# Gram matrices in two column halves, bias sums on GpSimd, and fewer filler steps in the first entry, in a four-layer convolution and attention kernel

## The chip, the cores and the metric

The kernel runs on one core of a Trainium2 chip. The metric is the device time in microseconds (us) of one execution, given as a median over runs. A profile of one execution is there too: a record of what each engine did. The engines are TensorE (PE; its weight loads are shown apart as PEld), VectorE (DVE), ScalarE (ACT), GpSimd (POOL) and SyncE (SP, which issues the transfers).

## The reference, cut to what matters

The input `x` is 8 batches of 512 channels by 1024 pixels in fp32. Four layers follow one another:

```python
# layer 0, MID = 64 channels: attention scaled by its largest singular value
f = relu(batchnorm(conv1x1(x, Wf, bf)))        # [8, 64, 1024]
g = relu(batchnorm(conv1x1(x, Wg, bg)))
h = conv1x1(x, Wh, bh)
z = einsum('bcn,bcm->bnm', f, g)
sigma = svd(z)[0]
x = x + conv1x1(einsum('bnm,bcm->bcn', z / sigma, h), Wv, bv)
# layer 1: group norm, attention with wq, wk, wv, wp, and x added
# layer 2: nonlocal attention over 128 channels, batch norm, and x added
# layer 3: 1x1 convolution of signs, batch norm, x added, a shifted PReLU
```

The kernel never forms `z`. Its singular values follow from the two 64x64 Gram matrices `f fT` and `g gT` of a batch, and `h zT` needs only `g hT`, also 64x64. Two batches make a pair: their 64 channels lie side by side on the 128 partitions. For the four pairs there are twelve Gram matrices of 128x128, of which only the two 64x64 blocks on the diagonal (one for each batch) have a meaning; the blocks off the diagonal would mix two batches.

## The kernel before, in words

**Stage 1, to about 100 us.** The 1x1 convolutions of layer 0 run for all eight batches (L1248), with statistics for the batch norm. Each batch is read in; two of them stay resident.

**Weight preparation and first entry, about 100 to 195 us.** This is where the change lies. Its pieces:

- `natural` (L1214) transposes the weights q, k, v. `product` (L1288) multiplies two of them: `wu` from k and q, and `wo` from p and v. A filler step of it is one 128x128 by 128x512 fp32 product, which the profile shows as two records[...].
- `relu` (L1370, on ACT) finishes f and g of a batch. `turned_pair` and `turn` (transposes at L1142, copies on ACT at L1146 and on DVE at L1148) turn a pair so that pixels lie on the partitions, in 8 tiles.
- `gram` (L1342) sums over the 8 tiles: eight 128x128 products of full width into a wide PSUM tile, with one `yield` after four. DVE multiplies the result with `mask2`, which zeroes the off-diagonal blocks, into `gm[j][:, i, :]` (L1351).
- `chain` finds the singular value of a pair by repeated squaring. Each step is two 128x128 products (`products`, L1029 and L1030), an eviction (L1043 to L1051), and now and then a trace sum (`total`, L1060) whose reciprocal scales the next eviction. The first pair's chain, `chain(jl, True)`, runs here; `jl` is pair 3, for batch 6 is the first in the order.
- `scale_z` makes a tile `rep` under the tag `absw` and reads it in four products with the identity (shown at L1202).
- `biases` makes two row vectors, `bu` and `bo`. It makes a tile `part` under the same tag `absw`; with it each weight's four tiles are scaled by a bias column and summed on DVE (one L1313 and three L1315 each), and then four products with a column of ones (L1322) sum over the partitions. `bo` also goes into `bvo`, which every entry adds.
- `sums_u` makes the Strassen-Winograd sums of `wu`.

All but the first pair's own steps are strung together in one generator, `filler()`, called `todo`. Its order is: natural v, product wu, Gram matrix 2 of the first pair, scale_z, then for the three other pairs their turns and Gram matrices with the steps of `biases` and `sums_u` taken in between, then product wo. A `yield` ends a filler step. The main body takes steps from `todo` by `next(todo)`: five at first, then after every step of the first chain one, two or four, then in the first batch's entry `entering(0)` by the list (2, 3, 3, 3, 4, 4, 6), and then what is left.

**What sets the order.** In the block with `tc.manual_schedule` PE's instructions run in just the order in which the program writes them; a wait of one holds up all that follow. DVE, ACT and POOL also run their own queues in order.

**The first entry** (`entering(0)`, which goes through `enter`): L290 makes the first batch's weights `pv` from a Gram tile; four visits, each of two products into two banks (L412) and on DVE, for each bank, an add (L421), statistics (L424), and once a visit an aggregate (L426). Then the group sums L433, small DVE steps, L440, a reciprocal root (L233 to L235, with a power on POOL), eight scalings of the batch into `h` (L463), and two sums `hs` for the Strassen-Winograd products (L327, L328). From there the main loop starts: its product terms at L388 are of `h` with `wu` and of `hs` with `su`. The chains of the other pairs run inside the main loop, between its products.

Of the kernel before, what the change touches and what calls it, by code (L numbers as in the profile page):

```python
# [8 lines left out]
F32 = mybir.dt.float32  # L9
# [3 lines left out]
ALU = mybir.AluOpType  # L13
# [3 lines left out]
P = 128  # L17
B = 8
C = 512
N = 1024  # L20
CC = C // P
NT = N // P
# [3 lines left out]
MID = 64  # L26
# [59 lines left out]
def kernel(  # L86
# [17 lines left out]
    nc = tc.nc  # L104
    mm = nc.tensor.matmul
# [11 lines left out]
    def wide():  # L117
        return psum["wide"].tile([P, N], F32, tag="wide", name="wide")
# [4 lines left out]
    def bank():  # L123
        return psum["bank"].tile([P, HF], F32, tag="bank", name="bank")
# [20 lines left out]
    def side(i):  # L145

        return slice(i * MID, (i + 1) * MID)
# [13 lines left out]
    a1 = early.enter_context(tc.tile_pool(name="a1", bufs=1))  # L161
# [10 lines left out]
    def block_ones(size, value, name):  # L172

        n = P // size
        member = const.tile([P, n], F32, tag=name + "_m", name=name + "_m")
        nc.vector.tensor_reduce(
            member, ident.rearrange("p (g j) -> p g j", j=size), AX.X, ALU.add
        )
        t = const.tile([P, n, size], F32, tag=name, name=name)
        nc.vector.tensor_scalar(  # L180
            t, member.unsqueeze(2).to_broadcast([P, n, size]), value, None, ALU.mult
        )
        return t.rearrange("p g j -> p (g j)")

    mask2 = block_ones(MID, 1.0, "mask2")
# [36 lines left out]
    def vec(name):  # L222
        return ct[:, COL[name] : COL[name] + CC]
# [20 lines left out]
    r_dram = [dram.tile([4, N // 4], F32, name=f"r_dram{i}") for i in range(2 * B)]  # L244
    f_dram = [dram.tile([P, HF], F32, name=f"f_dram{b}") for b in range(B)]
    gm = [keep.tile([P, 3, P], F32, tag=f"gm{j}", name=f"gm{j}") for j in range(NPAIR)]
    sw3 = wpool.tile([P, CC, C // 2], F16, tag="sw3", name="sw3")
    round3 = const.tile([P, 1], F32, tag="round3", name="round3")
    nc.gpsimd.memset(round3, ROUND)
# [616 lines left out]
    def entering(n):  # L866

        b = order[n]
        f = load_f(b)

        def steps():
            while b // 2 not in ready:
                next(behind)
            if b % 2 == 0:
                for i in (b, b + 1):
                    pvs[i] = weights0(i)
            yield
            yield from enter(resident[b], f, pvs.pop(b), 2 if n else CC)

        return steps()  # L880
# [423 lines left out]
    def biases():  # L1304

        part = a1.tile([P, 2, C], F32, tag="absw", name="part")
        for j, (w, v) in enumerate(((nat["k"], vec("L1_conv_bq")), (sbw["p"], bvc))):
            t = part[:, j, :]  # L1310
            for k in range(CC):
                if k == 0:
                    nc.vector.tensor_scalar(t, w[:, 0, :], v[:, 0:1], None, ALU.mult)  # L1313
                else:
                    nc.vector.scalar_tensor_tensor(  # L1315
                        t, w[:, k, :], v[:, k : k + 1], t, ALU.mult, ALU.add
                    )
                yield False
        for j, dst in enumerate((bu, bo)):
            ps = bank()  # L1320
            for i in range(CC):
                mm(  # L1322
                    out=ps[:, i : i + 1],
                    lhsT=part[:, j, bass.ts(i, P)],
                    rhs=ones1,
                    start=True,
                    stop=True,
                )
            if dst is bu:
                nc.vector.tensor_copy(bu, ps[:, 0:CC])  # L1330
            else:
                nc.vector.tensor_tensor(bo, ps[:, 0:CC], vec("L1_conv_bp"), ALU.add)
            yield True
        nc.vector.tensor_tensor(bvo, bo, vec("L0_conv_bv"), ALU.add)
# [2 lines left out]


    def gram(j, i, lt, rhs):
        ps = wide()  # L1340
        for t in range(NT):
            mm(  # L1342
                out=ps[:, 0:P],
                lhsT=lt[:, t, :],
                rhs=rhs[:, t, :],
                start=t == 0,
                stop=t == NT - 1,
            )
            if t == NT // 2 - 1:
                yield  # L1350
        nc.vector.tensor_tensor(gm[j][:, i, :], ps[:, 0:P], mask2, ALU.mult)  # L1351
        yield

    def turned_pair(j):
# [7 lines left out]
    def grams(j):  # L1362
        for ft, gt in turned_pair(j):
            yield
        for i, lt, rhs in ((0, ft, ft), (1, gt, gt), (2, ht_pair[j], gt)):
            yield from gram(j, i, lt, rhs)

    def relu(b, i):
        t = (fs, gs)[i][b]
        nc.scalar.activation(t, t, AF.Relu, bias=bi0[:, i : i + 1], scale=sc0[:, i : i + 1])  # L1370
        if i == 0:
            nc.sync.dma_start(out=f_dram[b], in_=t)
# [10 lines left out]
    ps = bank()  # L1383
# [5 lines left out]
    ps = bank()  # L1389
# [35 lines left out]
    def filler():  # L1425

        yield from natural("v", "k")
        load_w("p", w_p, [P, CC, C], a1, tag="v")  # L1430
        yield from product(nat["q"], nat["k"], wu, True)
        yield from gram(jl, 2, ht_pair[jl], gtl)
        scale_z()
        yield
        between = biases()
        sums = sums_u()
        for j in rest:
            for _ in grams(j):
                next(sums, None)
                yield  # L1440
                if next(between, None):
                    yield
        yield from product(nat["v"], sbw["p"], wo, False)

    todo = filler()
# [3 lines left out]
        pass  # L1449
    for i, t in ((0, ftl), (1, gtl)):  # L1450
        for _ in gram(jl, i, t, t):
            pass

    relus = iter([(2 * j + k, i) for j in rest for i in range(2) for k in range(2)])
    with tc.manual_schedule(engines={mybir.EngineType.PE}):
        steps = entering(0)
        for k, _ in enumerate(chain(jl, True)):

            for _ in range(4 if k == 3 * NSTEP + 3 else 2 if k % 3 == 1 or k == 0 else 1):
                next(todo, None)  # L1460
            for args in (next(relus, None),):
                if args:
                    relu(*args)
        for n in (2, 3, 3, 3, 4, 4, 6):
            next(steps)
            for _ in range(n):
                next(todo, None)
        for _ in todo:
            pass
# [195 lines left out]
```

## Time and profile before

| | us |
|---|---|
| median of three runs | 1898.24 |
| lowest, highest | 1897.3, 1898.89 |
| span of the profiled execution | 1896.9 |

In the profiled execution the mean granted clock of PE is 0.998 of full speed. Busy times over the span are given in the page's first part; here are those groups of the stretch that the change touches.

| group | count | where |
|---|---|---|
| L1342, Gram products | 192 records, one every 111.6 ns within a group | 109 to 171 us |
| L1029 and L1030, first chain | pairs of records, 0.38 us a product | 114 to 158 us |
| L1288, wu and wo | 0.86 us a product | 103 to 187 us |
| L412, the entry's products | four groups of 1.13 us | 161 to 174 us |

How to read the lines: "PE" is the engine, "L1342" the line of the kernel, then the operation, what it writes and what it reads, and for a timeline the start and the length in us first and the idle time before it, with what ended it, last. In a timeline neighbouring instructions of one kind are drawn together with a count, and the length of such a group is from the start of its first to the end of its last. In the list of groups the numbers after the bar are the busy time in us, the mean of one instruction in ns, and the idle time of the engine just before.

### The profile page before, as it was taken

What the parts mean: (1) busy time and instruction counts of PE and PEld (TensorE: products, weight loads), DVE (VectorE), ACT (ScalarE), POOL (GpSimd) and SP (SyncE); (2) the same over time, 40 slices, a digit from 0 to 9 for tenths busy, and PEclk for the clock granted to TensorE, in tenths of its full rate; (3) what the DMA queues carried; (4) which work ended last, traced back from release to release, by engine and by line L of the source; (5) the groups of instructions that cost most, each with busy time, mean ns of one, the idle gap of its engine ahead of it and who ended that gap; (6) DMA issues with size and microseconds to landing.
All of it is one profiled execution on the core that took longest, in us unless ns stands there. A gap on an engine that the chain in (4) does not pass through costs nothing.

```text
span 1896.9 us, 16376 instructions
## 1 busy us (share of the span) xinstructions
PE 1878.3 (99%) x6178; PEld 976.1 (51%) x6178; DVE 1097.5 (58%) x1762; ACT 511.4 (27%) x811; POOL 225.7 (12%) x176
## 2 busy tenths in 40 slices
PE   9999999999999999999999999999999999999997
PEld 3366556544745446444645446544645455544653
DVE  3256576448664677338663675457753775466547
ACT  2142222034312432035202421144202521234013
POOL 0000111201121011200121001200130011101121
PEclk9999999999999999999999999999999999999999
DMA  8420000002000020002000110002000200000001
GB/s 314 168 78 6 1 6 12 1 12 89 17 1 0 34 72 12 1 12 89 18 0 0 42 65 12 0 23 78 12 1 12 89 12 0 1 34 22 12 0 47
DMA packets 25203, 66.52 MB, mean 35 GB/s; under 512 B 3552, under 2 KB 4764, under 8 KB 24476
## 3 DMA queue, kind: packets, MB, share of 16 engines
q1 hardware_dynamic: 24188, 64.96, 9.4%
q8 instruction: 51, 0.84, 0.2%
q10 hardware_dynamic: 864, 0.43, 0.1%
q14 instruction: 36, 0.29, 0.0%
q0 software_dynamic: 64, 0.00, 0.0%
HBM read 46.44 MB, written 18.94 MB: 34 GB/s over the span
## 4 chain that ended last, share of the span: by engine, by line
PE 98%; DVE 1%; ACT 0%; DMA 0%; issue 0%; POOL 0%; ACTq 0%; DVEq 0%
PE bank L388 46%; PE bank L557 20%; PE bank L958 6%; PE bank L806 6%; PE bank L1248 5%; PE bank L658 3%; PE bank L675 3%; PE bank L412 2%; PE bank L698 1%; PE wide L1288 1%; PE bank L1029 1%; PE wide L1342 1%; PE bank L1030 1%; PE quad L1142 1%; PE bank L829 0%; PE bank L1060 0%
## 5 line engine op out<-in xcount | busy, mean ns | idle before, releaser
L557 PE MATMUL bank<-e,vt 128*128 128x512 f32 x768 | 333.8, 592 | 0.0
L557 PEld LDWEIGHTS bank<-e,vt 128*128 128x128 f32 x768 | 145.0, 190 | 175.4 <-issue 173.4
L388 PE MATMUL bank<-ut,h 128*128 128x512 f32 x384 | 182.3, 597 | 0.0
L345 DVE TENSOR_TENSOR e<-bank,e 128x512 f32<-128x512 f32 x128 | 87.8, 686 | 81.0 <-PE bank L388 80.3
L388 PE MATMUL bank<-us,hs 128*128 128x512 f32 x256 | 121.5, 597 | 0.3 <-DVE us L317 0.3
L388 PEld LDWEIGHTS bank<-ut,h 128*128 128x128 f32 x384 | 71.4, 190 | 95.6 <-issue 84.5
L958 PE MATMUL bank<-e,tpg 128*128 128x512 f32 x256 | 114.7, 595 | 0.0
L806 PE MATMUL bank<-tpg 128*128 128x512 f32 x256 | 114.6, 592 | 0.0
L813 ACT ACTIVATE e<-bank 128x512 f32<-128x512 f32 x128 | 76.4, 597 | 128.5 <-PE bank L806 128.5
L360 POOL TENSOR_TENSOR e<-e 128x512 f32<-128x512 f32 x32 | 44.2, 1381 | 412.5 <-ACT e L339 144.1
L388 PE MATMUL bank<-wo,h 128*128 128x256 f32 x384 | 91.9, 382 | 0.0
L388 PE MATMUL bank<-h,wu 128*128 128x512 f32 x192 | 90.4, 593 | 0.1
L818 DVE TENSOR_TENSOR esum<-esum,e 128x1024 f32<-128x1024 f32 x48 | 58.8, 1225 | 54.5 <-ACT e L813 54.5
L345 DVE TENSOR_TENSOR vt<-bank,vt 128x512 f32<-128x512 f32 x64 | 44.1, 689 | 65.5 <-PE bank L388 64.7
L806 PEld LDWEIGHTS bank<-tpg 128*128 128x128 f32 x256 | 48.6, 190 | 60.7 <-issue 60.5
L958 PEld LDWEIGHTS bank<-e,tpg 128*128 128x128 f32 x256 | 48.1, 190 | 60.4 <-issue 60.3
L388 PEld LDWEIGHTS bank<-wo,h 128*128 128x128 f32 x384 | 71.6, 190 | 11.5 <-issue 2.5
L360 POOL TENSOR_TENSOR ut<-ut 128x512 f32<-128x512 f32 x16 | 21.8, 1365 | 465.3 <-ACT ut L341 465.3
L388 PEld LDWEIGHTS bank<-us,hs 128*128 128x128 f32 x256 | 47.1, 190 | 52.9 <-issue 47.8
L686 ACT ACTIVATE sg<-xt,rb 128x512 f16<-128x512 f32 x64 | 45.3, 718 | 100.7 <-DVE xt L677 97.1
L1248 PE MATMUL bank<-xt,fg 128*64 128x512 f32 x256 | 59.9, 616 | 4.4 <-DMA fg<-in_w_fg 4.4
L658 PEld LDWEIGHTS bank<-tpg,xt 128*128 128x128 f32 x512 | 59.5, 192 | 7.2 <-issue 7.2
(333 smaller groups left out, 2968.1 us busy)
## 6 DMA issues: line engine op xcount, KB each, us to landing
xt<-in_x SPq DMA_DIRECT2D x55, 512.0 KB
out<-both SPq DMA_DIRECT2D x63, 256.0 KB
rfull<-r_dram SPq DMA_DIRECT2D x15, 512.0 KB
f_dram<-f SPq DMA_DIRECT2D x8, 256.0 KB
fb<-f_dram SPq DMA_DIRECT2D x8, 256.0 KB
w<-in_w SPq DMA_DIRECT2D x1, 1024.0 KB
q<-in_w_q SPq DMA_DIRECT2D x1, 1024.0 KB
k<-in_w_k SPq DMA_DIRECT2D x1, 1024.0 KB
```

What stands on the lines that cost most here:

```text
L345: nc.vector.tensor_tensor(dst, ps, u, ALU.add)
L360: nc.gpsimd.tensor_tensor(c22, c22, c12, ALU.add)
L388: mm(out=ps[:, q * w : (q + 1) * w], lhsT=lt(ka, kb, q, k), rhs=rhs(ka, kb, q, k), start=first and q == 0 and k == 0, stop=last and k == 1 ...
L557: mm(out=ps, lhsT=a[:, t, bass.ts(r_, P)], rhs=e[t], start=first and t == 0, stop=last and t == NTH - 1, skip_group_check=True,)
L658: mm(out=ps[:, i, :], lhsT=xt[:, cc, bass.ts(4 * h + i, P)], rhs=sbw["tpg"][:, cc, 2 * P : 3 * P], start=cc == 0, stop=cc == CC - 1,)
L675: mm(out=ps, lhsT=sbw["z"][:, bass.ts(oc, P)], rhs=att, start=True, stop=True)
L686: nc.scalar.activation(sg[:, cc, :], xt[:, cc, half(h)], AF.Sign, bias=rb3[:, cc : cc + 1])
L806: mm(out=ps, lhsT=pt[:, 0, bass.ts(t, P)], rhs=tt[:, 0, half(h)], start=True, stop=True,)
L813: nc.scalar.activation(e[:, half(h)], ps, AF.Exp, scale=float(P) ** -0.5)
L818: nc.vector.tensor_tensor(esum, esum, e, ALU.add)
L958: mm(out=banks[h], lhsT=gt[:, t, :], rhs=es[t][:, half(h)], start=t == 0, stop=t == NT - 1,)
L1248: mm(out=banks[i][side(h), :], lhsT=w0[i][:, cc, :], rhs=xt[:, cc, half(h)], start=cc == 0, stop=cc == CC - 1,)
```

## The change

There are four parts.

1. `gram` takes one bank instead of a wide tile. For each of the eight tiles it issues two 64x64 products, one for each batch of the pair, into its own half of the array's columns and of the bank's partitions. It has no `yield` halfway. The two diagonal blocks are copied to `gm`, one by DVE and one by ACT. The off-diagonal blocks of `gm` are zeroed once, by four memsets on POOL at the start.
2. Around the first pair's own two Gram matrices the loop takes a step from `todo` after each.
3. `biases` scales and sums on POOL: a scaling into a tile `term`, with one buffer, and an add. It yields once for each weight, not once for each of its tiles.
4. The list of filler steps in the first entry is (1, 2, 2, 2, 2, 3, 4), 16 in all, where it was 25.

```diff
     gm = [keep.tile([P, 3, P], F32, tag=f"gm{j}", name=f"gm{j}") for j in range(NPAIR)]
+    for g in gm:
+        nc.gpsimd.memset(g[:, 0:2, :].rearrange("p i c -> p (i c)"), 0.0)
...
             for k in range(CC):
-                if k == 0:
-                    nc.vector.tensor_scalar(t, w[:, 0, :], v[:, 0:1], None, ALU.mult)
-                else:
-                    nc.vector.scalar_tensor_tensor(
-                        t, w[:, k, :], v[:, k : k + 1], t, ALU.mult, ALU.add
-                    )
-                yield False
+                to = a1.tile([P, C], F32, tag="term", name="term") if k else t
+                nc.gpsimd.tensor_scalar(to, w[:, k, :], v[:, k : k + 1], None, ALU.mult)
+                if k:
+                    nc.gpsimd.tensor_tensor(t, t, to, ALU.add)
+            yield False
...
     def gram(j, i, lt, rhs):
-        ps = wide()
+
+        ps = bank()
         for t in range(NT):
-            mm(
-                out=ps[:, 0:P],
-                lhsT=lt[:, t, :],
-                rhs=rhs[:, t, :],
-                start=t == 0,
-                stop=t == NT - 1,
-            )
-            if t == NT // 2 - 1:
-                yield
-        nc.vector.tensor_tensor(gm[j][:, i, :], ps[:, 0:P], mask2, ALU.mult)
+            for k in range(2):
+                mm(
+                    out=ps[side(k), 0:MID],
+                    lhsT=lt[:, t, side(k)],
+                    rhs=rhs[:, t, side(k)],
+                    start=t == 0,
+                    stop=t == NT - 1,
+                )
+        for k in range(2):
+            to, of = gm[j][side(k), i, side(k)], ps[side(k), 0:MID]
+            if k:
+                nc.scalar.copy(to, of)
+            else:
+                nc.vector.tensor_copy(to, of)
         yield
...
         for _ in gram(jl, i, t, t):
-            pass
+            next(todo)
...
-        for n in (2, 3, 3, 3, 4, 4, 6):
+        for n in (1, 2, 2, 2, 2, 3, 4):
```

## The prediction

> **What bounds the kernel now.** I read first the page's busy shares and its chain of work that ended last:
>
> ```profile
> PE 1878.3 (99%) x6178; PEld 976.1 (51%) x6178; DVE 1097.5 (58%) x1762; ACT 511.4 (27%) x811; POOL 225.7 (12%) x176
> ...
> PE 98%; DVE 1%; ACT 0%; DMA 0%; issue 0%; POOL 0%; ACTq 0%; DVEq 0%
> ```
>
> TensorE is the bound over the whole span; all its idle time is 1896.9 − 1878.3 = 18.6 us. So PE work taken away is gained, unless PE then waits. The change touches only 109 to 191 us (weight preparation and the first batch's entry), so I read that stretch next, in the timeline of PE (start, us, instruction, count of records, idle before):
>
> ```profile
> 109.24 2.03 PE L1342 MATMUL wide<-ft 128*128 128x128 f32 x16
> 111.75 2.02 PE L1342 MATMUL wide<-gt 128*128 128x128 f32 x16 [0.47 <-DVE gm L1351]
> 114.15 0.49 PE L1029 MATMUL bank<-gm 128*128 128x128 f32 x2 [0.39 <-DVE gm L1351]
> ...
> 133.74 1.06 PE L1202 MATMUL bank<-ident,rep 128*128 128x128 f32 x8
> ...
> 158.43 1.13 PE L290 MATMUL bank<-wv,gm 64*128 64x512 f32 x4
> ...
> 181.40 0.28 PE L440 MATMUL bank<-dev,gmat 128*128 128x4 f32 x2
> 181.54 5.40 PE L1288 MATMUL wide<-p,nat_v 128*128 128x512 f32 x12
> 186.78 1.88 PE L388 MATMUL bank<-h,wu 128*128 128x512 f32 x4
> ...
> 191.15 1.88 PE L388 MATMUL bank<-hs,su 128*128 128x512 f32 x4
> ```
>
> PE is packed here; only the turn into the chain at 111 to 114 us shows waits. An fp32 product is two records, so a Gram matrix (8 products) is 16. Then the timeline of VectorE over the entry, which feeds PE:
>
> ```profile
> 174.28 0.75 DVE L421 SCALAR_TENSOR_TENSOR xt<-bank,bvo,xt 128x512 f32<-128x512 f32 x1 [0.70 <-PE bank L412]
> 175.07 0.69 DVE L424 BATCH_NORM_STATS2 st<-xt 128x6 f32<-128x512 f32 x1
> ...
> 177.42 0.17 DVE L432 TENSOR_TENSOR mv<-mv,bo 128x4 f32<-128x4 f32 x1
> ...
> 184.51 3.74 DVE L463 TENSOR_SCALAR h<-xt,r_r,bi 128x512 f32<-128x512 f32 x8
> ...
> 189.42 1.23 DVE L328 TENSOR_TENSOR hs<-h,hs 128x1024 f32<-128x1024 f32 x1
> ```
>
> One visit (a quarter of the channels) takes 174.28 to 177.42 = 3.1 us of DVE. After L440 the second term (hs, su) needs reciprocal root, eight L463 and L327/L328, all on DVE: they end at 189.42 + 1.23 = 190.65, that is 9.3 after L440 at 181.40. PE reaches that term at 191.15: DVE is ahead of PE by only half a microsecond. This is the point that decides here.
>
> [...] it has one tiled group amid full-size ones, L829:
>
> ```profile
> 280.98 0.16 PEld L829 LDWEIGHTS bank<-esum,ones 128*32 128x32 f32 x8 [0.33 <-issue]
> ...
> 281.55 0.30 PEld L1029 LDWEIGHTS bank<-cur 128*128 128x128 f32 x2 [0.41 <-issue]
> ```
>
> [...] the same Pool add has means from 1264 to 1381 ns in different rows.
>
> ```profile
> L360 POOL TENSOR_TENSOR vt<-vt 128x512 f32<-128x512 f32 x16 | 20.2, 1264 | 141.2 <-ACT vt L339 141.1
> L360 POOL TENSOR_TENSOR ut<-ut 128x512 f32<-128x512 f32 x16 | 21.8, 1365 | 465.3 <-ACT ut L341 465.3
> ```
>
> **The change, part by part.**
>
> *Gram matrices.* Before: 16 records, one every 111.6 ns within a group of L1342, = 1.79 us (the groups show 1.95 to 2.03, with the last record drawn to its end). After: 16 products of 64x64, two side by side. By array work, half of 1.79 = 0.9; [...] if issue is no faster than today's 109 ns per 128-column transpose product, 16 × 0.109 = 1.75. I take 0.99, since L829's eight loads in 0.16 us show issue far below 109 ns. Twelve Gram matrices then save 12 × 0.80 = 9.6 us. The mode changes cost: around L829 the weight loads going in and coming out are not hidden behind the products before them; of the 0.33 and 0.41 that PEld idles there I estimate that 0.15 and 0.20 stop the products, 0.35 in all. The Gram matrices form 11 such islands: 3.9. Net 5.7 us less PE work. The two evictions on DVE and ACT instead of one on DVE run beside each other, 0.2 to 0.3 each, and off PE but for the first pair; there ACT has relus of 0.71 queued ahead of the copies. Two L1288 products (1.7 us) now lie in those waits. By ACT's queue I put the chain's first product, L1029, at 113.7 instead of 114.15. The four Pool memsets stand at the start, with Pool idle till long after: nothing; without that cover some microseconds of Pool, before 100 us.
>
> *Bias sums on Pool.* They leave DVE: two L1313 at 0.48 and six L1315 at 0.74, 5.4 us, off the path. On Pool they are eight scalings and six adds. "part" shares its buffer with "rep", so all but one of them wait for the transposes L1202 of "rep". Before, those ran 133.74 to 134.8; with two Gram halves and two products gone from ahead of them they end at about 130.3. Pool starts at 130.6: seven scalings, six adds. No one-input scaling is in the trace. Below, a bare 0.6 us (DVE's own 0.48 at a lesser rate); above, as dear as the add, 1.27. [...] Sum: 7 × 0.92 + 6 × 1.27 + 13 × 0.08 between instructions[...] = 15.8, so bu's sum is done at about 138.9 and bo's at 146.4.
> Now "yield False" comes once per bias, not once per k, so L1322 (bu) stands only three filler steps on, and PE reaches it at 136.1. PE's order is fixed as written, so everything behind it waits: 2.8 us. Then chain, a Gram matrix and the trace sum follow, PE reaches bo's L1322 at 142.3 and waits till 146.4, 4.1 us, and leaves at 147.3. Nearly 7 us of idle time on PE, where before the DVE sums were ready in time.
>
> *The way to the entry.* After 147.3 PE has seven Gram matrices × 0.99, six islands × 0.35, seven chain products × 0.45, three trace sums × 0.15, four turns × 0.87, three wo products × 0.86, and 0.6 of short waits: 6.9 + 2.1 + 3.2 + 0.5 + 3.5 + 2.6 + 0.6 = 19.4. So L290 comes at about 166.7, where it was at 158.43. It is later though less work is ahead of it, since fewer fillers are given to the entry and so more of the total lies ahead.
>
> *The entry.* With 16 filler steps instead of 25 the entry is no longer PE's but DVE's: from L290 some 3.3 us to the first L421 (product, copy out, first L412 with a filler step or two between), four visits × 3.1 = 12.4, 0.25 for the last small steps: L433 at L290 + 16.0 = 182.7. Behind it three L1288 products (2.6 us) stand ahead of L440 as written, which DVE's small work between (0.6) would not need: L440 at 185.6. The second term is 9.3 later: 194.9, against 191.15. **Plus 3.7 us.** In this stretch PE has only some 17 us of work for 28 of time; the saved work ends as idle time in front of L433, L440 and L388. Behind 191.15 nothing is changed, so this shift carries to the end. The profiled span 1896.9 + 3.7 = 1900.6; the median shown is 1.3 above the span (1898.24), so 1901.9. About 0.2% (3.8 us) is what a measurement of this kernel can tell from no change.
>
> **Rivals.**
>
> *B, Pool is quick.* With scalings at 0.6[...] and a shorter start, bo's sum comes at 143.4, L290 three microseconds sooner: +0.7, 1899. If the sums are never late (from about 0.4 us a scaling on, with adds shorter too), PE comes through bo at 140.5, and the whole is −3: 1895. For: the one-input price is open. Against: six adds at the trace's 1.264 alone are 7.6.
>
> *C, Gram products are bound by issue.* 16 × 0.109 = 1.75: no gain, and the mode changes stay. The nine Gram matrices that lie ahead of L290 on the path after the chain's start then cost 9 × 0.76 = 6.9 more, part of it inside Pool's wait but most not: about 1908. For: transposes, also 128 columns, never start faster in the trace. Against: the column halves of L1248 run in pairs. It decides if a 64-column product costs over 90 ns.
>
> *D, Pool is slow.* Scalings at 1.27 and twice the meetings: 7 × 0.35 + 1 = 3.5 more, 1905.4. The mechanism is the same wait, longer; the point is a scaling above 1.1.
>
> *E, the edit does not do what it says:* if the two halves were run one after the other in the array, that is C.
>
> **Chances.** A, as worked out, 0.45 (1900 to 1904); B 0.27 (1894.5 to 1900, of it 0.06 below 1894.4); C 0.13; D 0.15. Within 0.2% are B's other 0.21 and half of A, 0.22: 0.43. Slower are half of A, C and D: 0.51. The range 1896.5 to 1908 leaves out B's quick end (0.1) and C's slow end (0.06).
>
> **What would show it.** In the profile after: Gram groups of about 0.5 us per eight products; idle PE time of 2 to 4 us before each L1322, released by Pool; Pool scalings near 0.92; L290 near 166.7; idle PE before L433 and L440; the (hs, su) term near 195. If PE is not idle before L1322, or L290 comes before 162, the forecast is wrong and B holds; if Gram matrices take 1.7 us, C.

## The result and the profile after

The changed kernel takes 1908.06 us (median of 4 runs, 1907.62 to 1909.16) against 1898.39 us beside it: a ratio of 1.0054, with a 95% interval of 1.0041 to 1.0066. It is slower by 9.7 us. The forecast was 1901.9, so the sign of the shift was right, its size was not, and the time lies 0.06 us above the upper end of the stated range. The profiled execution took 1907.69 us, its span is 1905.9.

In the changed kernel line numbers are two higher up to the entry and the chain: L1029 is now L1031, L290 is L292, L412 is L414, L433 and L440 are L435 and L442, L388 is L390. The scalings on Pool are L1315, the adds L1317, the products with the column of ones are still L1322, and the Gram products L1344. First the busy shares and the chain that ended last:

```profile
PE 1876.3 (98%) x6370; PEld 973.0 (51%) x6370; DVE 1092.7 (57%) x1754; ACT 514.3 (27%) x823; POOL 247.1 (13%) x194
...
PE 97%; POOL 1%; DVE 1%; ACT 1%; issue 0%; DMA 0%; DVEq 0%; ACTq 0%; POOLq 0%
```

PE is busy 2.0 us less than before, but idle 1905.9 − 1876.3 = 29.6 us instead of 18.6. And POOL, with 0% of the chain before, now has 1% of it. The timeline of PE shows where:

```profile
133.75 1.15 PE L1344 MATMUL bank<-ft 128*64 128x64 f32 x32 [0.58 <-DVE gt L1150]
134.95 0.49 PE L1031 MATMUL bank<-cur 128*128 128x128 f32 x2
...
140.48 1.86 PE L1322 MATMUL bank<-ones,part 128*128 128x1 f32 x8 [4.82 <-POOL part L1317]
...
143.34 1.98 PE L1344 MATMUL bank<-gt 128*64 128x64 f32 x32
...
149.51 1.86 PE L1322 MATMUL bank<-ones,part 128*128 128x1 f32 x8 [2.82 <-POOL part L1317]
151.31 1.97 PE L1344 MATMUL bank<-gt,ht 128*64 128x64 f32 x32
...
157.66 1.15 PE L1344 MATMUL bank<-ft 128*64 128x64 f32 x32
158.64 1.10 PE L1344 MATMUL bank<-gt 128*64 128x64 f32 x32
...
171.94 1.35 PE L292 MATMUL bank<-wv,gm 64*128 64x512 f32 x4
...
187.71 0.39 PE L435 MATMUL bank<-mv,gmat 128*128 128x4 f32 x2 [1.48 <-DVE mv L434]
...
190.61 0.28 PE L442 MATMUL bank<-dev,gmat 128*128 128x4 f32 x2
...
194.44 2.45 PE L390 MATMUL bank<-h,wu 128*128 128x512 f32 x4 [2.58 <-DVE h L465]
...
200.29 1.88 PE L390 MATMUL bank<-hs,su 128*128 128x512 f32 x4
```

Both waits on Pool are there, 4.82 and 2.82 us, and the (hs, su) term comes at 200.29 instead of 191.15: 9.1 us later. The span grew by 9.0, so the whole loss lies ahead of this term. Two things are new. The first wait is longer than the 2.8 that was forecast, the second shorter than 4.1, since the work ahead of it was slow. And the same instructions have two lengths: a Gram matrix is 1.15 us at 133.75 and at 157.66, but 1.98 at 143.34 and 1.97 at 151.31; L1322 takes 1.86. The windows show why (the columns are the busy times of PE, PEld, DVE, ACT and POOL, then the granted clock of PE as a share of full speed; the last two are of the transfers):

```profile
125.00:140.00 15.00, 9.96 (x116) 7.86 (x114) 9.13 (x23) 3.13 (x10) 9.79 (x7) 0.92 0.00 1
140.00:155.00 15.00, 11.69 (x99) 11.14 (x100) 2.33 (x13) 1.31 (x5) 8.91 (x7) 0.51 0.00 0
155.00:172.00 17.00, 16.86 (x259) 13.94 (x256) 8.95 (x38) 8.28 (x20) 0.00 (x0) 1.00 0.01 2
```

From 140 to 155 us PE was granted half its clock. Now Pool's timeline, and VectorE's at the entry:

```profile
129.85 1.80 POOL L1315 TENSOR_SCALAR part<-nat_k,ct 128x512 f32<-128x512 f32 x1 [15.17 <-PE bank L1204]
131.63 1.56 POOL L1315 TENSOR_SCALAR part<-p,bvc 128x512 f32<-128x512 f32 x1
...
148.20 1.26 POOL L1317 TENSOR_TENSOR part<-part,term 128x512 f32<-128x512 f32 x1
```

```profile
193.75 3.74 DVE L465 TENSOR_SCALAR h<-xt,r_r,bi 128x512 f32<-128x512 f32 x8
```

A scaling takes 1.56 us, more than the add with its two inputs (1.26). The run of work starts at 129.85, behind "rep" as forecast, and ends at 149.46: 19.6 us. The entry is as forecast: L292 to L435 15.8 us (16.0), L442 another 2.9 (2.9), the second term another 9.7 (9.3). In these 9.7 us PE waits for h at L390, for 2.58 us, and the products behind the wait take 2.45 us instead of 1.88: this too is a slow stretch, with a granted clock of 0.50 from 195.76 to 199.18 us (last section).

One caution for all comparisons below: the work ahead of this stretch scatters from run to run. The power on POOL for the first batch norm begins between 102.04 and 103.38 us in the kernels that don't move it, in no order that follows their edits. So stretches are measured between two instructions of one trace, and medians are taken for the whole.

### The profile page after: what moved, and what is told of

It reads as the page before. It is cut to its first block, busy times and chain, and to the rows that moved or that the text cites. A ratio compares the mean times of both kernels' runs of the same rounds, so it can differ in the third digit from the quotient of the medians.

```text
span 1905.9 us, 16783 instructions
## 1 busy us (share of the span) xinstructions
PE 1876.3 (98%) x6370; PEld 973.0 (51%) x6370; DVE 1092.7 (57%) x1754; ACT 514.3 (27%) x823; POOL 247.1 (13%) x194
## 4 chain that ended last, share of the span: by engine, by line
PE 97%; POOL 1%; DVE 1%; ACT 1%; issue 0%; DMA 0%; DVEq 0%; ACTq 0%; POOLq 0%
PE bank L390 46%; PE bank L559 20%; PE bank L960 6%; PE bank L808 6%; PE bank L1250 5%; PE bank L660 3%; PE bank L677 3%; PE bank L414 2%; PE bank L700 1%; PE wide L1290 1%; PE bank L1031 1%; PE bank L1032 1%; PE bank L1344 0%; PE bank L831 0%; PE quad L1144 0%; POOL term L1315 0%
## 5 line engine op out<-in xcount | busy, mean ns | idle before, releaser
L390 PE MATMUL bank<-ut,h 128*128 128x512 f32 x384 | 182.3, 597 | 0.0
L390 PE MATMUL bank<-us,hs 128*128 128x512 f32 x256 | 121.5, 597 | 0.3 <-DVE us L319 0.3
L390 PEld LDWEIGHTS bank<-ut,h 128*128 128x128 f32 x384 | 71.4, 190 | 95.6 <-issue 84.5
L390 PE MATMUL bank<-h,wu 128*128 128x512 f32 x192 | 91.6, 600 | 2.6 <-DVE h L465 2.6
L390 PE MATMUL bank<-wo,h 128*128 128x256 f32 x384 | 91.9, 382 | 0.0
L390 PEld LDWEIGHTS bank<-wo,h 128*128 128x128 f32 x384 | 71.6, 190 | 11.5 <-issue 2.5
L390 PEld LDWEIGHTS bank<-us,hs 128*128 128x128 f32 x256 | 47.1, 190 | 52.9 <-issue 47.8
```

Of the source, the lines that this page charges most:

```text
L390: mm(out=ps[:, q * w : (q + 1) * w], lhsT=lt(ka, kb, q, k), rhs=rhs(ka, kb, q, k), start=first and q == 0 and k == 0, stop=last and k == 1 ...
```

## The experiments

Theory P: the loss is PE's wait for the Pool sums, made longer by dear scalings, and the half clock that follows the wait (0.51 from 140 to 155 us). Theory R: it is the narrow Gram products, their mode changes (from full products to narrow ones and back) and the entry bound by VectorE, and the Pool wait only fills slack.

**1. Sums back on VectorE, same places.**

```diff
-                to = a1.tile([P, C], F32, tag="term", name="term") if k else t
-                nc.gpsimd.tensor_scalar(to, w[:, k, :], v[:, k : k + 1], None, ALU.mult)
...
+                    nc.vector.tensor_scalar(t, w[:, 0, :], v[:, 0:1], None, ALU.mult)
...
+                    nc.vector.scalar_tensor_tensor(
+                        t, w[:, k, :], v[:, k : k + 1], t, ALU.mult, ALU.add
+                    )
             yield False
```

> The changed kernel with its bias sums put back on VectorE, at the same places in the order (one yield for each weight). Theory P (the late Pool sums and the clock that PE loses while it waits for them make the loss): PE reaches L1322 without a wait, the 4.8 and 2.8 us of idle time and 2.3 us of slow products go, L292 comes near 162 instead of 171.9, and since the entry behind it is as long as before, the median falls by 9.9 to about 1898.2. Theory R (narrow products, mode changes and a DVE-bound entry make the loss, the wait for Pool only fills slack): at most 3 us are gained, 1905 or more.

Measured: 1902.07 us (ratio to before 1.002, interval 1.0012 to 1.0028). That is 6.0 below the changed kernel, between the theories, and the trace of PE tells why:

```profile
137.31 1.05 PE L1324 MATMUL bank<-ones,part 128*128 128x1 f32 x8 [1.29 <-DVE part L1317]
139.66 0.77 PE L1031 MATMUL bank<-cur 128*128 128x128 f32 x2 [1.29 <-DVE cur L1047]
...
140.78 1.98 PE L1346 MATMUL bank<-gt 128*64 128x64 f32 x32
```

With L1322's group (here L1324) so soon after the start of the sums, even VectorE is late: both sums and the other fillers' copies stand ahead of what PE needs, twice 1.29 us are lost, and the granted clock is 0.50 from 139.1 to 149.3. So the place of the yield is a cause by itself, whichever engine sums. My expectation that nothing would wait here was wrong.

**2. Sums on Pool, but farther from their use.** One indentation:

```diff
-            yield False
+                yield False
```

> The changed kernel, sums still on Pool, but with a yield for each of a weight's four tiles as before, so that PE does Gram matrices and turns between the start of the sums and L1322. Theory P: scalings still take 1.56 us and the sums still end near 149.5, but PE no longer waits and keeps its clock: within 1 us of the version with the sums on VectorE, about 1898.5. Theory R: 1905 or more. A third (Pool's reads hold up VectorE[...]): 2 us or more above the version with the sums on VectorE, with longer DVE rows between 130 and 150 us.

Measured: 1897.96 us (ratio 0.9998, 0.9989 to 1.0006): 10.1 us gained by the order alone. The trace of PE:

```profile
145.80 1.02 PE L1322 MATMUL bank<-ones,part 128*128 128x1 f32 x8
...
149.35 1.05 PE L1322 MATMUL bank<-ones,part 128*128 128x1 f32 x8 [0.81 <-POOL part L1317]
...
162.00 1.35 PE L292 MATMUL bank<-wv,gm 64*128 64x512 f32 x4
```

Pool is as slow as ever (a scaling takes 1.56 or 1.57 us, its last add ends at 149.3), but PE has Gram matrices and turns to do meanwhile. L292 comes at 162.00, 9.9 us sooner. Theory R is out: all the narrow products and mode changes are still there. That this version is 4 us below number 1 also speaks against a large loss by contention between Pool and VectorE; the pair that would settle its size, these far yields with the sums on VectorE, was not run.

**3. PE kept busy while it waits.** In `biases`, ahead of each L1322 group:

```diff
             ps = bank()
+            for _ in range(5):
+                mm(out=ps, lhsT=ident, rhs=wv2, start=True, stop=True)
+            ps = bank()
```

> The changed kernel with five idle products (identity by wv2, 0.86 us each, into a bank that nobody reads) ahead of each of the two L1322 groups, so that PE works while it waits. Pool's sums end as before, near 140.4 and 149.4. Theory P with its clock term: the granted clock between 140 and 155 us is 1 instead of 0.51, L1322 and the Gram matrix behind it take 1.0 and 1.0 us instead of 1.8 and 1.9, and 2.3 us are gained, 1905.8. Without a clock term (the slow rows are those products' own): 1908 or slightly more.

Measured: 1906.62 us (1906.19 to 1908.99), 1.4 below the changed kernel by the medians. In the traces the stretch from bo's L1322 to L292, all of it free of Pool, shrinks from 171.94 − 149.51 = 22.4 to 170.60 − 150.56 = 20.0 us, by 2.4. PE and a window of this kernel:

```profile
150.56 1.05 PE L1325 MATMUL bank<-ones,part 128*128 128x1 f32 x8 [1.19 <-POOL part L1317]
151.54 1.15 PE L1347 MATMUL bank<-gt,ht 128*64 128x64 f32 x32
...
170.60 1.35 PE L292 MATMUL bank<-wv,gm 64*128 64x512 f32 x4
```

```profile
140.00:155.00 15.00, 13.27 (x123) 9.34 (x122) 3.67 (x17) 2.07 (x7) 9.88 (x8) 1.00 0.01 1
```

The clock is 1.00 where it was 0.51. The same instructions are short again, though they do the same work: the slow rows were the clock, and the clock fell because PE was idle. Its price is 2.4 us by the traces and 1.4 by the medians. In this trace Pool's run starts 1.0 us later than in the changed kernel's (130.87 against 129.85), ahead of anything that the edit adds, so the scatter is as large as the difference between the two.

**4. Fewer fillers ahead of L442.** List (1, 2, 2, 2, 2, 1, 6).

> The changed kernel with the entry's list of filler steps (1, 2, 2, 2, 2, 1, 6): one wo product instead of three stands ahead of L442, the others behind it. Theory (what stands ahead of L442 is on the path, since the entry is bound by VectorE): L442 comes 1.7 us sooner, and the median falls to about 1906.3. Rival (PE's work in the entry is the bound): no change, 1908.

Measured: 1906.65 us, 1.4 below. PE:

```profile
188.42 0.39 PE L435 MATMUL bank<-mv,gmat 128*128 128x4 f32 x2 [1.48 <-DVE mv L434]
...
199.07 1.98 PE L390 MATMUL bank<-hs,su 128*128 128x512 f32 x4 [0.29 <-DVE hs L330]
```

L435 to the (hs, su) term falls from 200.29 − 187.71 = 12.6 to 199.07 − 188.42 = 10.7, by 1.9; of this, 1.7 lie between L435 and L442, which now comes at 189.65. So what is written ahead of L442 is on the path, as the prediction said.

**5. The Gram part alone.** The kernel before, with only the new `gram` and the memsets.

> The kernel before with part 1 alone: Gram matrices in two 64-column halves with the zeroed tiles; bias sums on VectorE with their old yields, no extra filler in the first loop, the old list (2, 3, 3, 3, 4, 4, 6). Theory (the Gram part saves PE 5.7 us, of which the entry, then bound by VectorE, takes most back): no wait at L1322, L292 near 160, all wo products ahead of L442 so that L442 follows L435 by under 1 us, the (hs, su) term near 188.7 against 191.15, median about 1896. Rival 1 (the saved work is gained in full): 1892.6. Rival 2 (mode changes and two evictions eat the saving): 1898 or more.

Measured: 1896.53 us (ratio 0.9991, 0.9983 to 0.9999). Of the 5.7 us of work that the prediction estimates as saved, 1.7 arrive. Where the rest lies is seen in the entry, on PE:

```profile
178.35 0.39 PE L442 MATMUL bank<-dev,gmat 128*128 128x4 f32 x2 [0.84 <-DVE dev L439]
182.25 3.75 PE L390 MATMUL bank<-h,wu 128*128 128x512 f32 x4 [3.52 <-DVE h L465]
...
188.76 1.88 PE L390 MATMUL bank<-hs,su 128*128 128x512 f32 x4
```

PE waits 4.4 us for VectorE, and behind the wait its first four records take 3.75 instead of 1.88 us, at a granted clock of 0.50 (181 to 187 us). The (hs, su) term comes at 188.76, forecast 188.7.

**6. The Pool part alone.** The kernel before, with only the new sums and their yield.

> The kernel before with part 3 alone: bias sums on Pool, one yield for each weight. Theory: Pool starts near 135 us, its sums end near 145.6 and 154.6, PE waits 5 and 6 us for them ahead of the two groups of products with the column of ones, runs at about half clock behind each wait, and since the entry of the kernel before is packed on PE all of it carries to the end: about 1910. Rival (the entry is bound by VectorE here too and takes up to 7 us of delay without loss): about 1903.

Measured: 1912.26 us (ratio 1.0077, 1.0063 to 1.009), 14 us slower. On PE:

```profile
144.57 1.86 PE L1320 MATMUL bank<-ones,part 128*128 128x1 f32 x8 [5.06 <-POOL part L1315]
...
153.61 1.86 PE L1320 MATMUL bank<-ones,part 128*128 128x1 f32 x8 [3.55 <-POOL part L1315]
...
156.61 3.76 PE L1340 MATMUL wide<-gt 128*128 128x128 f32 x16
...
171.77 1.13 PE L290 MATMUL bank<-wv,gm 64*128 64x512 f32 x4
```

The waits are 5.1 and 3.6 us, and the full-width Gram matrix at 156.61 takes 3.76 us, at a granted clock of 0.50, where it took 1.95 to 2.03 before. L290 comes 13.3 later than before, and with an entry packed on PE all of that stays. The two waits are together 2.4 us shorter than I expected and the loss is 2.3 us larger: I had put the price of the half clock, which lasts from 144 to 161 us here, too low.

The two parts alone give −1.7 and +14.0, together 12.3, where the whole change gives 9.7. Parts 2 and 4, the filler steps in the first loop and the 16 steps in place of 25, were not run alone, so how this difference divides between them is open.

**7. The scalings as products of two tensors.**

```diff
-                nc.gpsimd.tensor_scalar(to, w[:, k, :], v[:, k : k + 1], None, ALU.mult)
+                nc.gpsimd.tensor_tensor(
+                    to, w[:, k, :], v[:, k : k + 1].to_broadcast([P, C]), ALU.mult
+                )
```

> The changed kernel with the eight scalings on Pool written as products of two tensors, the bias column repeated along the row, in place of a product with a column per partition. Theory P: what is dear is the scaling by a column (1.56 us); a product of two tensors costs what the adds cost, 1.26, so bo's sum ends 7 x 0.3 = 2.1 us sooner, and the median falls by 2.1 to about 1906.0. Rival: the price is one of the column or of the multiplication itself, 1.5 us or more as before: 1908.

Measured: 1904.62 us, beside 1897.69 for the kernel before (ratio 1.0036, 1.0022 to 1.005). So it is 6.9 above before, where the changed kernel is 9.7 above: 2.7 gained. Pool, and one line of VectorE:

```profile
133.50 1.37 POOL L1315 TENSOR_TENSOR term<-nat_k,ct 128x512 f32<-128x512 f32 x1
...
144.02 1.04 POOL L1315 TENSOR_TENSOR term<-p,bvc 128x512 f32<-128x512 f32 x1
145.13 1.26 POOL L1319 TENSOR_TENSOR part<-part,term 128x512 f32<-128x512 f32 x1
```

```profile
132.44 1.53 DVE L1427 TENSOR_TENSOR wu<-wu 128x512 f32<-128x512 f32 x1
```

The same scaling takes 1.04 us in this form, and 1.29 to 1.37 in three places, of which those at 129.90 and 133.50 start while VectorE has a product or sum of two tiles under way (129.60 to 130.29 and 132.44 to 133.97); bo's sum ends at 146.39, 3.1 sooner. It is the form "tensor by a column" that is dear on Pool (1.56 us), not the multiplication (1.04).

**8. A free tile for "rep".** `rep` takes the tag `hraw`, so that `part` is free from the start.

> The changed kernel with rep in a tile that is free by then (the tag hraw), so that part needn't wait for rep's transposes. Theory P: Pool starts near 100 us instead of 130 and has both sums done before PE comes to L1322, so the waits and the slow clock go, which is worth 9.9. But Pool runs in order, and the power of the first batch norm (L234, at 102.3 us) now has up to four bias operations of 1.26 to 1.56 ahead of it, and the relus wait for it: from nothing to 4.7 us given back. So 1898.2 to 1902.9, with L234 near 107 in the latter case. Rival (the sums would have been late wherever they start): 1906 or more.

Measured: 1902.32 us beside 1897.69 (ratio 1.0025, 1.0015 to 1.0035), at the far end of what was expected. Pool, and then PE:

```profile
99.44 1.58 POOL L1315 TENSOR_SCALAR part<-nat_k,ct 128x512 f32<-128x512 f32 x1 [87.54 <-ACT nat_k L1220]
...
106.88 0.73 POOL L234 TENSOR_TENSOR r_r<-r_v,minus_half 128x2 f32<-128x2 f32 x1
```

```profile
112.15 1.11 PE L1144 MATMUL quad<-ident,f 128*128 128x128 f32 x4 [6.12 <-ACT f L1375]
...
143.11 0.95 PE L1322 MATMUL bank<-ones,part 128*128 128x1 f32 x8
...
146.34 1.02 PE L1322 MATMUL bank<-ones,part 128*128 128x1 f32 x8
```

The waits at L1322 are gone. But five bias operations, where there was one, now stand in Pool's queue ahead of the power L234, which comes at 106.88 instead of 102.27; the relus wait for it, and PE waits 6.1 us for them. The shared tag, which looked like the fault, had kept Pool free for the power.

**9 and 10. A better order.** Number 9 joins experiments 2 and 4. Number 10 has the yields of experiment 2, two more of them ahead of the bo products, and moves three filler steps out of the chain, into the entry:

```diff
-            yield False
+                yield False
+            if j:
+                for _ in range(2):
+                    yield False
...
-            for _ in range(4 if k == 3 * NSTEP + 3 else 2 if k % 3 == 1 or k == 0 else 1):
+            for _ in range(4 if k == 3 * NSTEP + 3 else 2 if k in (0, 1, 4, 7, 10) else 1):
...
-        for n in (1, 2, 2, 2, 2, 3, 4):
+        for n in (1, 2, 2, 2, 3, 1, 9):
```

> The changed kernel with a yield for each tile in the bias sums (Pool has time) and the entry's list (1, 2, 2, 2, 2, 1, 6). Theory: the two edits act at different places, so the 1.4 us of the list come on top of 1897.96: 1896.5. Rival (PE is the bound once the Pool wait is gone): 1898.

> As the one before, and three filler steps are moved from the first pair's chain (one instead of two after its steps 13, 16 and 19) into the entry, list (1, 2, 2, 2, 3, 1, 9), with two more yields ahead of the bo products so that Pool's second sum is in time. Theory (the saved Gram time lies as idle time of PE in front of L435 and L390, and work moved there is free): L292 near 158, full clock from 155 to 190, the (hs, su) term near 186, median about 1893.5. Rival (the chain is bound by its own latency, so it doesn't end sooner with fewer fillers): 1896.5 or more.

Measured: 1895.84 us (ratio 0.999, 0.9981 to 0.9998) and 1893.85 us (ratio 0.9978, 0.9969 to 0.9986). The last beats both kernels, by 4.4 and 14.2 us. PE in it:

```profile
160.00 1.83 PE L292 MATMUL bank<-wv,gm 64*128 64x512 f32 x4
...
176.25 0.39 PE L435 MATMUL bank<-mv,gmat 128*128 128x4 f32 x2 [0.61 <-DVE mv L434]
...
177.72 4.54 PE L1290 MATMUL wide<-p,nat_v 128*128 128x512 f32 x10
182.10 1.88 PE L390 MATMUL bank<-h,wu 128*128 128x512 f32 x4
...
186.91 1.98 PE L390 MATMUL bank<-hs,su 128*128 128x512 f32 x4 [0.27 <-DVE hs L330]
```

The five wo products at 177.72 fill the time in which VectorE makes h; L390 follows at a granted clock of 1.00. L292 comes at 160.0 where I said 158: the chain now waits three times for its own evictions, 0.8 to 1.1 us each, so the rival, a chain bound by its latency, holds in part.

## Why the prediction was wrong

**Gram matrices: the size right, in part by luck.** 0.98 us from start to start (157.66 to 158.64) against 0.99. No trace of the kernel before shows the 0.99. The trace after has 32 records in the 0.98 us, 31 ns each, and at a clock of 0.50 the group is 1.98 us long instead of 1.15 at 1.00: it follows TensorE's clock, and the prediction's price by array work, 0.9, fits nearly as well. An island costs about 0.3 us, against 0.35: around the Gram matrix at 160.32 three gaps between starts are 0.1 us longer than elsewhere (160.00 to 160.32, to 161.40, to 161.73: 0.32, 1.08 and 0.33 us, where L1032 to L1062 at 291.01 is 0.23, Gram matrix to Gram matrix 0.98, and L1031 to L1032 at 156.82 0.23). Rivals C and E, no gain from the halves, are out, and so is B, the quick Pool.

**The entry: right.** Bound by VectorE, with its three stretches within 0.4 us (in the last one PE, slowed to a clock of 0.50, comes to the (hs, su) term 0.4 us after VectorE's end of hs, 199.88), and three products ahead of L442 on the path, which experiment 4 shows. Experiment 5 shows that the entry takes back most of the Gram gain.

**The step that failed is the price of a scaling on Pool, 0.92 us in the sum of 15.8.** A scaling took 1.56 us, outside the bounds of 0.6 and 1.27 that I set. The error was to hold that the two-input add bounds the one-input scaling from above. The 0.92 between them was not shown by any trace. The sums took 19.6 us instead of 15.8: **3.8 us**. The 15.8 hold 0.7 us, an estimate of mine, for meetings of Pool with VectorE; Pool needed 0.24: its first scaling took 1.80, beside a sum of two tiles on VectorE (129.52 to 130.21); the adds are 1.26 or 1.27 in all rows.

**A term that was missing: the clock.** I priced the idle time of PE as idle time only. Behind it PE ran at 0.50 to 0.51 of its clock. The part ahead of bo's L1322 cost nothing, since Pool set that time; the part behind it cost 2.4 us by the traces (experiment 3). The trace has the fall inside the wait of 4.82 us, 2.1 us after PE's last product (last section).

The sum: 3.7 as forecast + 3.8 + 2.4 = 9.9, against 9.7 measured; with the 1.4 that the medians of experiment 3 show for the clock it would be 8.9. The forecast's L292, 166.7, was 171.94 here, or 172.8 with the 0.9 by which this trace ran ahead of that of before in the stretch ahead: 6.1 late = 3.8 + 2.3. Of the rivals D was the nearest, "the same wait, longer", and its sign, a scaling above 1.1, came true; but it too stopped at 1905.4, with scalings at 1.27 and no term for the clock.

**What the prediction left half said.** It named the single yield as the reason why PE reaches L1322 so early, but weighed only Pool's price. Experiments 1 and 2 show the order as the greater cause: with the yield near, the kernel is 3.8 us over before even with its sums on VectorE; with it far, and the sums on slow Pool, it can't be told from before.

## What to carry to other kernels

Moving side work to a slow engine was free here only where its consumer stood far enough behind in the order of the engine that is the bound (1897.96 us with a yield for each tile, 1908.06 with one for each weight); count the steps between them, and count what the same queue must still do for others. Price an operation on GpSimd by its own row or not at all: a simpler operation isn't therefore a cheaper one (here 1.56 us for a scaling, 1.26 for an add of two tensors). And where the bound engine will wait for a few microseconds, look at the clock behind the wait: here it was 0.50 after waits of 4.82 and 2.82 us, and the work behind the second took 2.4 us more by the traces. Useful work put into the wait can save both, as in the last of the orders above.

## What was not expected of the hardware

- On GpSimd, 128x512 fp32 scaled by a column takes 1.56 us, the product with that column repeated along the row 1.04 (1.29 to 1.37 in three places, two of them beside VectorE operations with two inputs), and the add of two tensors 1.26.
- The granted clock fell from 1.00 to 0.50 after little idle time: 2.1 us into the first wait of the changed kernel, in the second of two waits of 1.29 us with 1 us of work between (experiment 1), and after one of 0.81 us (experiment 2, where it is 0.50 from 150.9 to 154.3). In experiment 1 it stayed at 0.50 until 149.3, through 9.6 us of work without a gap.
- In the trace of the changed kernel the changes of the clock from 130 to 202 us lie whole multiples of 3.41 us apart. These are windows of it, with the share of clock as the third number from the end:

```profile
137.00:138.00 1.00, 0.00 (x0) 0.00 (x0) 0.00 (x0) 0.00 (x0) 0.90 (x2) 0.87 0.00 0
...
154.00:155.00 1.00, 1.00 (x8) 1.00 (x7) 0.29 (x1) 0.27 (x1) 0.00 (x0) 0.60 0.00 0
...
195.00:196.00 1.00, 1.00 (x4) 0.49 (x3) 1.00 (x3) 0.00 (x0) 0.00 (x0) 0.88 0.00 0
...
199.00:200.00 1.00, 1.00 (x4) 0.42 (x3) 1.00 (x2) 0.00 (x0) 1.00 (x1) 0.91 0.00 0
```

  With 1.00 before and 0.50 behind, a share of 0.87 means half clock for 0.26 us of the 1 us, so the clock fell at 137.74; in the same way it rose at 154.80, fell at 195.76 and rose at 199.18. The distances are 17.06, 40.96 and 3.42 us, that is 5, 12 and 1 times 3.41, and in the traces of the experiments every slow stretch of this part of the kernel lasts about 3.4, 6.8, 10.2 or 17.1 us (10.2 and 3.4 in number 1, twice 3.4 in number 2, 6.8 in numbers 5 and 8, 17.1 in number 6; numbers 9 and 10 have none). The second fall came 1.3 us after PE had gone back to work. Whether the cost of a wait depends on where it falls among these points no run here shows, and 2.4 us need not hold for the next kernel. What decides at such a point is left open.
- VectorE and Pool were slower in some places where both were at work. In the changed kernel a 128x1 product of two columns on VectorE, 0.15 us before, took 0.82 beside a Pool add (133.16 to 134.42) and ended with it, at 134.44. On Pool's side it shows in the 1.80 us of the first scaling, against 1.56, and in the 1.29 to 1.37 of experiment 7, against 1.04. But a product of two tiles on VectorE at 132.36, inside a Pool scaling, kept its 0.68 us, so not every such pair waits.

```profile
133.62 0.82 DVE L1088 TENSOR_TENSOR r<-r 128x1 f32<-128x1 f32 x1
```
